# First keys on ScalarE, convolution steps ahead of turns, feed-forward bias two pairs later

## The chip, the core and the metric

The kernel runs on one core of one Trainium2 chip. The metric is the device time of one execution in microseconds (us). Matrix products run on TensorE (PE in the profile, PEld its weight loads), element-wise work on VectorE (DVE), ScalarE (ACT) and GpSimd (POOL); SyncE (SP) issues most of the DMAs. Each engine takes its instructions in the order in which the program was built.

## The reference

The input is x, 2 images of 256 channels on 56 x 56 points, in float32. Two layers act on it:

```python
# layer 0
x = x + conv_attention(group_norm(x))
# layer 1, on tokens of 256 values
t = to_tokens(x)
t = t + attention(layer_norm(t))
t = t + experts(layer_norm(t))
x = from_tokens(t)
```

`conv_attention` makes q, k and v by a 1 x 1 product and a depthwise 3 x 3 convolution, and lets every point attend to a 7 x 7 window (four heads with dilation 1, four with dilation 2), followed by a projection. `attention` is linear attention: with K = elu(k) + 1 and Q = elu(q) + 1 it sums K's products with v over all tokens of an image, and each query reads these sums (the message); a feed-forward net of 512 hidden values with Relu takes token and message. `experts` sends each token to two of eight feed-forward nets with Gelu.

## The kernel before, in words

The first image's convolutions and window attention come first (0 to about 420 us). Then `layer1` runs linear attention in two halves, one for each image; `half == 0` is the first image. Expert work fills gaps from about 795 us on, and is all there is from about 1440 us to the end.

**Keys.** `linear` (L1640) sets up a half. Its tokens are taken in pairs of 128-token tiles (12 pairs and a half tile in each image, `pairs`). `keys` (L266) is a generator with three parts per pair. Part one: statistics of the tile (`stats`, L246; its rstd is a VectorE instruction, L260, and a power on GpSimd, L261), the normalised tile xt (`norm`, L154, on VectorE), its turn by four transposes into pts (L278), copied to xT on ScalarE or VectorE by turns (`evac`, L178). Then up holds the scale and offset with which ScalarE changes t in place (L289); GpSimd adds b2 (L292). Part two: kp from xT and w_k (L297), and ks = elu(kp) + 1 by two ScalarE instructions (L242, L243) and one on VectorE (L244). Part three: kx adds ks times xt into PSUM (L309), and kacc adds ks on GpSimd (L314, L316). rs, up, st and mv come from a pool with three buffers (the pool `sm`), and so do the xt tiles (tag u); a fourth pair reuses the buffers of the first. For the first three pairs (`j < 3`, eager) norm and evac stand with high priority.

`all_keys` (L2105) yields after each part of each pair, in the order part two of a pair, part one of the next, part three of the one before. Behind yield 5 `layer1` calls `ln.feed()`, which is `prepare_feed_forward` (L1781): it centres fw2 (a sum wmean on VectorE, L1733, and a subtraction, L1735), makes the bias hb by 8 products (L1788), copies it (L1792) and scales two quarters of fw1 (L1794).

**Turns.** `steps` (L2144) then advances groups of four tiles through queries (q: pq and, in its second part, pd and qz), message (m: pm, then mts), feed-forward (f: p and py), routing (r) and scatters (P). Each string of `parts` is a turn; each letter takes the next piece of one of these.

**Convolution steps.** The second image's convolutions are left over as a generator, `Convolutions.run` (L496). A step (`fill` in the keys, letter k in `parts`) is two matmuls into py (L521, 448 or 280 columns), and a ScalarE copy into ypad (L527). Four steps fill one of two ypad halves; then 18 strips of 784 values follow, two on ScalarE (L561) and 16 on VectorE (L564, into yc), and one store of yc to DRAM on SP (L579). py has one PSUM bank, ypad two halves, yc two buffers. The strips have a low priority (LATE).

**What sets the order.** The framework orders the instructions of all engines by priority and by its own estimate of times, except TensorE's: under `manual_schedule` they stand as written, and what an engine has in front of it is fixed when the program is built. `tc.issue_after(x)` places instructions behind x. Loads, stores and spills stand on SP in one queue.

Of the kernel before, what the change touches and what calls it, by code (L numbers as in the profile page):

```python
# [13 lines left out]
F32 = mybir.dt.float32  # L14
AF = mybir.ActivationFunctionType
ALU = mybir.AluOpType
# [4 lines left out]
P = 128  # L21
# [40 lines left out]
NFS, NHS = 48, 5  # L62
NFI = 14
LEAD = 22
ENDING = (4, 6, 13, 15, 20)
XW = C + 4

# [58 lines left out]
def hybrid_kernel(ctx: ExitStack, tc: tile.TileContext, a: dict, out: bass.AP):  # L126
    nc = tc.nc
# [138 lines left out]
    def keys(tk, wk, sm, ps, bank, w_k, b2, kx, acc, n0, n, p, first, last, eager):  # L266


        t = tk.at(n0, n)[p]
        rows = p.stop - p.start  # L270
        mv, rs = stats(sm, t, tk.up[p, n0 : n0 + n], p)
        xt = wk.tile([P, 2, C + E], F32, name="xt", tag="u", bufs=3)[p, :, :C]
        pts = ps.tile([P, 2, 2 * P], F32, name="pts", tag="a")
        for k in range(n):
            with tc.high_priority() if eager else nullcontext():
                norm(xt[:, k, :], t[:, k, :], mv, rs, k)
            for ct in range(2):
                nc.tensor.transpose(  # L278
                    pts[:, ct, k * P : k * P + rows], xt[:, k, ct * P : (ct + 1) * P], ident[p, p]
                )  # L280
        xT = tk.turned(n0, n)[:, :, p] if n == 1 else tk.turned(n0, n)
        with tc.high_priority() if eager else nullcontext():
            evac(xT, pts[:, :, : n * rows])

        up = sm.tile([P, 2, 2], F32, name="up")[p]
        nc.vector.tensor_scalar(up[:, 0, :n], rs[:, :n], 1.0, None, ALU.add)
        nc.vector.scalar_tensor_tensor(up[:, 1, :n], mv[:, :n, 0], -1.0, rs[:, :n], ALU.mult, ALU.mult)
        for k in range(n):
            nc.scalar.activation(  # L289
                t[:, k, :], t[:, k, :], AF.Identity, bias=up[:, 1, k : k + 1], scale=up[:, 0, k : k + 1]  # L290
            )
        nc.gpsimd.tensor_tensor(t, t, b2[p].unsqueeze(1).to_broadcast([rows, n, C]), ALU.add)  # L292
        yield
        kps = bank()[p]
        for k in range(n):
            for ct in range(2):
                nc.tensor.matmul(  # L297
                    kps[:, k, :], xT[:, ct, k * rows : (k + 1) * rows], w_k[:, ct, :],
                    start=(ct == 0), stop=(ct == 1),
                )  # L300
        ks = wk.tile([P, 2, C], F32, name="ks", tag="mn")[p]
        elu1(
            wk, ks[:, :n, :].rearrange("p k c -> p (k c)"), kps[:, :n, :].rearrange("p k c -> p (k c)"),
            "k", 4, p,
        )
        yield
        for k in range(n):
            for hg in range(2):
                nc.tensor.matmul(  # L309
                    kx[:, hg, :], ks[:, k, hg * P : (hg + 1) * P], xt[:, k, :],  # L310
                    start=(first and k == 0 and hg == 0), stop=(last and k == n - 1), skip_group_check=True,
                )
        if first:
            nc.gpsimd.tensor_copy(acc, ks)  # L314
        else:
            nc.gpsimd.tensor_tensor(acc[p, :n, :], acc[p, :n, :], ks[:, :n, :], ALU.add)  # L316
        yield
# [20 lines left out]

    fp = [[dram.tile([KC, NH, 21, wide[s]], F32, name=f"fp{s}{k}") for k in range(3)] for s in range(2)]

    def project(dst, x_t, parts, wpr):

        for ct in range(2):
            nc.tensor.matmul(
                dst[:, ct * P : (ct + 1) * P], x_t[:, ct, :], ident,
                start=(ct == 0), stop=False, is_transpose=True, skip_group_check=True,
            )
        for k, (o, s) in enumerate(parts):
            nc.tensor.matmul(  # L349
                dst, o, wpr[:, s, :], start=False, stop=(k == len(parts) - 1), skip_group_check=True  # L350
            )

    anchors = {}

    def bias_tables(sp, ac, pp):

# [1283 lines left out]
    def linear(ph, tk, half, behind=None):  # L1640
# [11 lines left out]
        kp, sm, tp, wqp, wp, wk, lp = (pools[k] for k in "estqwkl")  # L1652
        ps_a, ps_h, ps_q = pool("p3pa", 2, space=PSUM), pool("p3ph", 3, space=PSUM), pool("p3pq", 2, space=PSUM)
# [12 lines left out]
        with tc.issue_after(anchors["final"]) if behind else nullcontext(), tc.high_priority():  # L1666
            w_k = load("w_k", rows("L1_attn_Wk"), [P, 2, C], kp)
            b2 = load("b2", a["L1_attn_b2"].partition_broadcast(P), [P, C], kp)
# [429 lines left out]
        if half == 0:  # L2098
            kx = ps_h.tile([P, 2, C], F32, name="kx", tag="h")
        else:  # L2100
            kx = ps_k.tile([P, 2, C], F32, name="kx", tag="kx")
        acc = wk.tile([P, 2, C], F32, name="kacc", tag="z")
        pairs = [(n0, 2, slice(0, P)) for n0 in range(first, last, 2)] + [(NA - 1, 1, own)]

        def all_keys():  # L2105


            bank = lambda: (ps_h if half else ps_q).tile(
                [P, 2, C], F32, name="kp", tag="h" if half else "q"
            )  # L2110
            live = {}
            for i in range(len(pairs) + 2):
                for k in (1, 0, 2):
                    j = i - k
                    if j == i and j < len(pairs):
                        live[j] = keys(
                            tk, wk, sm, ps_a, bank, w_k, b2, kx, acc, *pairs[j], j == 0, j == len(pairs) - 1, j < 3
                        )
                    if 0 <= j < len(pairs):
                        next(live[j])  # L2120
                        yield
# [8 lines left out]
        def keep():  # L2130
# [8 lines left out]
            wk=wk, ps_h=ps_h, ps_q=ps_q, ps_a=ps_a, ps_k=ps_k, late=late,  # L2139
            bank=lambda: ps_a.tile([P, 512], F32, name="pp", tag="a"),  # L2140
# [23 lines left out]
    def layer1(whole, tk, conv_ctx=None, conv=None, behind=None):  # L2164
# [5 lines left out]
        def fill(n=1):  # L2170
            for _ in range(n):
                next(conv, None)
# [6 lines left out]
        with ExitStack() as ph:  # L2179
            ln = linear(ph, tk, 0, behind)  # L2180
            with tc.manual_schedule(engines={mybir.EngineType.PE}):
                for i, _ in enumerate(ln.keys()):
                    if i == 5:
                        ln.feed()
                    if i < 3 or (i > 8 and i % 6 == 1):
                        fill()
                merging = ln.close()
                prepared = ln.router()
                parts = (
                    "qkwkxkwkxqwkxqq", "mkqkmkqk", "mkqkfmqffkfkff",  # L2190
                    "mqfkfPPPPmkqfkrfrff", "mqfkpPPPPfmqfrfrff", "mqfpPPPPfmqfrfrff",
                    "mfpPPPPfmfrfrff", "fpPPPPffrffrf", "rpPPPPr", "pPPPP",
                )
                todo = steps(ln, order[:early1], parts, {"k": conv, "w": merging, "x": prepared})
                for part in islice(todo, sum(len(t) for t in parts[:7])):
                    pass
                for _ in conv:
                    pass
            ln.keep()
            if conv_ctx:  # L2200
                conv_ctx.close()
            ex = Experts(whole, tk)
            late = ExitStack()
            if run == 0:
                ln.late(late)
            with tc.manual_schedule(engines={mybir.EngineType.PE}):
                for part in islice(todo, len(parts[7]) + 1):
                    pass

            def ending():  # L2210

                next(todo)
                yield
                for part in islice(todo, 4):
                    pass
                next(todo)
                yield
                table = ex.full_tiles(ln.bank()[:, :E], ln.ones)
                next(table)
                next(todo)  # L2220
                yield
                for part in todo:
                    pass
                yield
                for _ in table:
                    pass

            ending = ending()
            if run:
                for _ in ending:  # L2230
                    pass
# [17 lines left out]
        if run == 0:  # L2249
            with ExitStack() as ph:  # L2250
                bank = Banks()
# [7 lines left out]
                with tc.manual_schedule(engines={mybir.EngineType.PE}):  # L2259
                    for i, what in enumerate(att.run()):  # L2260
                        if i in ENDING:
                            next(ending, None)
                        if i == ENDING[-1]:
                            xc = experts()
                        if i >= LEAD and (what == "scores" or what == "values" or what == "end"):
                            with tc.issue_after(anchors["table"]) if first else nullcontext():
# [168 lines left out]
```

## Time and profile before

| | us |
|---|---|
| three runs | 2000.4, 2003.97, 2013.45 |
| median | 2003.97 |
| profiled execution, its own time | 2003.56 |
| its span, first to last instruction | 2001.8 |
| granted TensorE clock, mean | 0.969 |

| stage (us) | PE busy | DVE busy | ACT busy | clock |
|---|---|---|---|---|
| 300 to 400 | 92.57 | 82.98 | 38.62 | 1.00 |
| 400 to 500 | 82.51 | 85.20 | 36.27 | 0.90 |
| 500 to 550 | 44.43 | 44.38 | 20.50 | 0.97 |
| 550 to 600 | 44.91 | 44.83 | 17.12 | 0.93 |
| 600 to 650 | 49.26 | 37.83 | 21.56 | 1.00 |
| 1500 to 1600 | 100.00 | 20.69 | 26.54 | 1.00 |

How to read it: the profile shows one execution. A busy time is the time in which an engine executes; idle time is put down to the instruction that ended the wait. A float32 matmul of the program is two records in the profile. "clock" is the share of full speed that TensorE was granted. In a row of waits the numbers are the total in us, how often, and the longest; in a row of the timeline they are start and length in us, and in brackets the idle time ahead and what ended it. Rows of windows give for each engine busy time and count.

### The profile page before, as it was taken

What the parts mean: (1) busy time and instruction counts of PE and PEld (TensorE: products, weight loads), DVE (VectorE), ACT (ScalarE), POOL (GpSimd) and SP (SyncE); (2) the same over time, 40 slices, a digit from 0 to 9 for tenths busy, and PEclk for the clock granted to TensorE, in tenths of its full rate; (3) what the DMA queues carried; (4) which work ended last, traced back from release to release, by engine and by line L of the source; (5) the groups of instructions that cost most, each with busy time, mean ns of one, the idle gap of its engine ahead of it and who ended that gap; (6) DMA issues with size and microseconds to landing.
All of it is one profiled execution on the core that took longest, in us unless ns stands there. A gap on an engine that the chain in (4) does not pass through costs nothing.

```text
span 2001.8 us, 27731 instructions
## 1 busy us (share of the span) xinstructions
PE 1842.0 (92%) x9996; PEld 1308.3 (65%) x9996; DVE 1094.2 (55%) x2733; ACT 704.5 (35%) x1331; POOL 582.2 (29%) x634
## 2 busy tenths in 40 slices
PE   6999898988889996899989989999899999999996
PEld 3545354556555654566668756567688888888885
DVE  6978988888887746555557434554531212121221
ACT  2333324324434323445536433323322232323332
POOL 4630221025102444111126311445422222222221
PEclk9999999989999996999999999999999999999998
DMA  4753432340001534654474211114577676766995
GB/s 112 160 138 110 133 92 75 111 146 17 25 38 42 157 85 145 193 152 134 129 201 127 56 34 37 48 57 132 156 230 200 188 199 189 198 190 195 299 279 161
DMA packets 200153, 268.85 MB, mean 134 GB/s; under 512 B 30953, under 2 KB 158615, under 8 KB 199761
## 3 DMA queue, kind: packets, MB, share of 16 engines
q1 hardware_dynamic: 167920, 223.95, 37.0%
q0 software_dynamic: 19728, 27.54, 7.5%
q10 hardware_dynamic: 12352, 15.43, 2.2%
q8 instruction: 83, 1.36, 0.3%
q14 instruction: 70, 0.57, 0.1%
HBM read 200.19 MB, written 70.95 MB: 135 GB/s over the span
## 4 chain that ended last, share of the span: by engine, by line
PE 47%; DMA 4%; DVE 4%; ACT 3%; issue 1%; POOL 1%; SPq 0%; ACTq 0%; DVEq 0%; POOLq 0%
PE ph L1600 13%; PE py L1618 13%; PE p L1935 4%; PE x L1618 2%; DMA y<-yt,idi 2%; PE x L1600 2%; PE py L1951 2%; PE po L658 2%; DMA xr<-xs 1%; PE kx L309 1%; PE kp L297 1%; PE x L349 1%; PE pm L1905 1%; PE s_ps L644 1%; PE px L1569 1%
## 5 line engine op out<-in xcount | busy, mean ns | idle before, releaser
L1600 PE MATMUL ph<-xe,w1e 128*128 128x256 f32 (+1 forms) x1448 | 312.1, 371 | 15.3 <-ACT hT L1604 9.4
L1618 PE MATMUL py<-w2e,hT 128*128 128x256 f32 x1392 | 311.5, 379 | 0.0
L1604 ACT ACTIVATE hT<-ph,sv 128x256 f32<-128x256 f32 (+1 forms) x362 | 165.7, 462 | 393.4 <-PE ph L1600 386.1
L1600 PEld LDWEIGHTS ph<-xe,w1e 128*128 128x128 f32 x1448 | 262.6, 191 | 55.0 <-ACT hT L1604 11.2
L1618 PEld LDWEIGHTS py<-w2e,hT 128*128 128x128 f32 x1392 | 260.2, 190 | 33.2 <-issue 0.2
L167 POOL DMA_INDIRECT y<-yt,idi x101 | 160.2, 1587 | 325.4 <-DVE yt L1624 186.9
L571 DVE SCALAR_TENSOR_TENSOR yc<-ypad,w,yc 128x1120 f32<-128x1120 f32 x144 | 202.8, 1412 | 26.4 <-ACT yc L561 18.5
L261 POOL TENSOR_TENSOR rs<-rs,mhalf 128x2 f32<-128x2 f32 (+3 forms) x90 | 72.1, 805 | 323.6 <-DVE rs L260 292.7
L521 PE MATMUL py<-x_sb,wq 128*128 128x448 f32 (+1 forms) x384 | 153.8, 532 | 5.4 <-ACT ypad L527 3.8
L648 ACT ACTIVATE p<-s_ps 112x952 f32<-112x952 f32 (+5 forms) x88 | 102.1, 1160 | 154.6 <-PE s_ps L644 96.0
L1552 DVE CAST idi<-xr 128x2 int32<-128x2 f32 (+1 forms) x53 | 9.8, 184 | 258.6 <-DMA xr<-xs 258.4
L649 DVE TENSOR_TENSOR p<-p,tab 112x952 f32<-112x952 f32 (+5 forms) x88 | 122.0, 1389 | 45.5 <-ACT p L648 39.6
L542 PE MATMUL pc<-ypad,diag 128*128 128x448 f32 x324 | 131.9, 548 | 0.0
L1624 DVE SCALAR_TENSOR_TENSOR yt<-py,eq,yt 128x256 f32<-128x256 f32 x87 | 41.8, 482 | 156.6 <-PE py L1618 156.4
L1582 POOL TENSOR_SCALAR yt<-b2e,eq 128x256 f32<-128x256 f32 x101 | 50.4, 505 | 251.5 <-DMA b2e<-in_L_ffn_b 209.0
L167 POOL DMA_INDIRECT xs<-row,si x98 | 100.5, 1026 | 71.9 <-DVE si L2082 41.9
L521 PEld LDWEIGHTS py<-x_sb,wq 128*128 128x128 f32 x384 | 71.7, 197 | 67.1 <-issue 56.8
L564 DVE SCALAR_TENSOR_TENSOR yc<-ypad,w,yc 128x784 f32<-128x784 f32 x96 | 101.8, 1077 | 4.2 <-ACT yc L561 3.6
L658 PE MATMUL po<-p,v 98*32 98x170 f32 (+5 forms) x960 | 71.2, 379 | 29.1 <-issue 12.6
L542 PEld LDWEIGHTS pc<-ypad,diag 128*128 128x128 f32 x324 | 59.8, 191 | 52.4 <-issue 48.7
L1935 PE MATMUL p<-m2T,fw 128*128 128x512 f32 (+2 forms) x224 | 93.8, 542 | 0.0
L1935 PE MATMUL p<-xT,fw 128*128 128x512 f32 (+1 forms) x208 | 92.7, 568 | 0.0
(391 smaller groups left out, 2891.1 us busy)
## 6 DMA issues: line engine op xcount, KB each, us to landing
w1e<-in_L_ffn_W SPq DMA_DIRECT2D x53, 1024.0 KB
w2e<-in_L_ffn_W SPq DMA_DIRECT2D x53, 1024.0 KB
yd<-yc SPq DMA_DIRECT2D x24, 784.0 KB
ld<-yd SPq DMA_DIRECT2D x28, 448.0 KB
xr<-xs SPq DMA_DIRECT2D x48, 260.0 KB
b2e<-in_L_ffn_b SPq DMA_DIRECT2D x53, 128.0 KB
t<-td SPq DMA_DIRECT2D x12, 512.0 KB
y<-t ACTq DMA_DIRECT2D x24, 256.0 KB
```

The lines of the kernel that those rows point to most:

```text
L167: ins = nc.gpsimd.indirect_dma_start(out=dst[:, :], out_offset=bass.IndirectOffsetOnAxis(ap=index, axis=0), in_=src, in_offset=None, **kw,)
L521: nc.tensor.matmul(py[:, :n, :], self.wq1[:, ct, oc * P : (oc + 1) * P], self.x_sb[:, ct, (q0 + g0) * WW : (q0 + g0 + n) * WW], start=(ct ...
L542: nc.tensor.matmul(pc, diag[:, tap, :], ypad[:, dy : dy + SHARE, dx : dx + WW], start=(tap == 0), stop=(tap == 8),)
L564: nc.vector.scalar_tensor_tensor(yc[:, y0:y1, :], src, w, yc[:, y0:y1, :], ALU.mult, ALU.add)
L571: nc.vector.scalar_tensor_tensor(yc[:, y0:y1, :], src, w, yc[:, y0:y1, :], ALU.mult, ALU.add)
L648: nc.scalar.activation(p[:nk, :, :n], s_ps[:nk, :, :n], AF.Exp)
L649: nc.vector.tensor_tensor(grid(p), grid(p), table[:nk], ALU.mult)
L658: nc.tensor.matmul(dst[hs] if w is None else den[hs], v[:nk, hs] if w is None else w[:nk, :], p[:, h, :, o : o + q.shape[2]], start=first ...
L1600: nc.tensor.matmul(p1, x.w1[:, ct, j * P : (j + 1) * P], x.xe[:, ct, :], start=(ct == 0), stop=(ct == 1),)
L1604: nc.scalar.activation(hT[:, j, :], p1, AF.Gelu, bias=x.sv[:, 4 + j : 5 + j])
L1618: nc.tensor.matmul(py, hT[:, j, h * P : (h + 1) * P], x.w2[:, j, :], start=(j == 0), stop=(j == NJ - 1),)
L1935: nc.tensor.matmul(p1[:, :w], fw1[:, k, oc * P : (oc + 1) * P], rhs, start=(k == 0), stop=(k == 3))
```

## The change

Four things change. The normalised tiles of the first three pairs of the first image are made by ScalarE (Identity with scale rs and offset -mean times rs, which is the second value of up; up's second value is therefore made ahead, in both halves); only these pairs keep the high priority. One convolution step goes ahead of the keys together with the end of the half image in hand, behind the last projection; the others in the keys go in front of the turn of a later pair instead of behind it, and there are nine instead of eight (`FILLS`). In `parts`, the third, fourth and fifth turn lose one step each, and the first and second gain one each, in front of the messages; the ninth step in the keys is the other. `ln.feed()` is called behind yield 11 instead of 5 in the first half.

```diff
--- before.py
+++ after.py
@@ -62,6 +62,7 @@
 NFS, NHS = 48, 5
 NFI = 14
 LEAD = 22
+FILLS = (0, 2, 12, 18, 24, 27, 33)
 ENDING = (4, 6, 13, 15, 20)
 XW = C + 4
 
@@ -271,8 +272,16 @@
         mv, rs = stats(sm, t, tk.up[p, n0 : n0 + n], p)
         xt = wk.tile([P, 2, C + E], F32, name="xt", tag="u", bufs=3)[p, :, :C]
         pts = ps.tile([P, 2, 2 * P], F32, name="pts", tag="a")
+        up = sm.tile([P, 2, 2], F32, name="up")[p]
+        with tc.high_priority() if eager else nullcontext():
+            nc.vector.scalar_tensor_tensor(up[:, 1, :n], mv[:, :n, 0], -1.0, rs[:, :n], ALU.mult, ALU.mult)
         for k in range(n):
-            with tc.high_priority() if eager else nullcontext():
+            if eager:
+                with tc.high_priority():
+                    nc.scalar.activation(
+                        xt[:, k, :], t[:, k, :], AF.Identity, bias=up[:, 1, k : k + 1], scale=rs[:, k : k + 1]
+                    )
+            else:
                 norm(xt[:, k, :], t[:, k, :], mv, rs, k)
             for ct in range(2):
                 nc.tensor.transpose(
@@ -282,9 +291,7 @@
         with tc.high_priority() if eager else nullcontext():
             evac(xT, pts[:, :, : n * rows])
 
-        up = sm.tile([P, 2, 2], F32, name="up")[p]
         nc.vector.tensor_scalar(up[:, 0, :n], rs[:, :n], 1.0, None, ALU.add)
-        nc.vector.scalar_tensor_tensor(up[:, 1, :n], mv[:, :n, 0], -1.0, rs[:, :n], ALU.mult, ALU.mult)
         for k in range(n):
             nc.scalar.activation(
                 t[:, k, :], t[:, k, :], AF.Identity, bias=up[:, 1, k : k + 1], scale=up[:, 0, k : k + 1]
@@ -338,6 +345,8 @@
 
     fp = [[dram.tile([KC, NH, 21, wide[s]], F32, name=f"fp{s}{k}") for k in range(3)] for s in range(2)]
 
+    anchors = {}
+
     def project(dst, x_t, parts, wpr):
 
         for ct in range(2):
@@ -346,11 +355,9 @@
                 start=(ct == 0), stop=False, is_transpose=True, skip_group_check=True,
             )
         for k, (o, s) in enumerate(parts):
-            nc.tensor.matmul(
+            anchors["projected"] = nc.tensor.matmul(
                 dst, o, wpr[:, s, :], start=False, stop=(k == len(parts) - 1), skip_group_check=True
-            )
-
-    anchors = {}
+            ).ins
 
     def bias_tables(sp, ac, pp):
 
@@ -2114,7 +2121,7 @@
                     j = i - k
                     if j == i and j < len(pairs):
                         live[j] = keys(
-                            tk, wk, sm, ps_a, bank, w_k, b2, kx, acc, *pairs[j], j == 0, j == len(pairs) - 1, j < 3
+                            tk, wk, sm, ps_a, bank, w_k, b2, kx, acc, *pairs[j], j == 0, j == len(pairs) - 1, j < 3 and half == 0
                         )
                     if 0 <= j < len(pairs):
                         next(live[j])
@@ -2179,16 +2186,19 @@
         with ExitStack() as ph:
             ln = linear(ph, tk, 0, behind)
             with tc.manual_schedule(engines={mybir.EngineType.PE}):
+                fill()
+                with tc.issue_after(anchors["projected"]) if behind else nullcontext():
+                    fill()
                 for i, _ in enumerate(ln.keys()):
-                    if i == 5:
+                    if i == 11:
                         ln.feed()
-                    if i < 3 or (i > 8 and i % 6 == 1):
+                    if i in FILLS:
                         fill()
                 merging = ln.close()
                 prepared = ln.router()
                 parts = (
-                    "qkwkxkwkxqwkxqq", "mkqkmkqk", "mkqkfmqffkfkff",
-                    "mqfkfPPPPmkqfkrfrff", "mqfkpPPPPfmqfrfrff", "mqfpPPPPfmqfrfrff",
+                    "qkwkxkwkxqwkxqqk", "mkqkmkqkk", "mkqkfmqffkfff",
+                    "mqfkfPPPPmkqfrfrff", "mqfpPPPPfmqfrfrff", "mqfpPPPPfmqfrfrff",
                     "mfpPPPPfmfrfrff", "fpPPPPffrffrf", "rpPPPPr", "pPPPP",
                 )
                 todo = steps(ln, order[:early1], parts, {"k": conv, "w": merging, "x": prepared})
```

## The prediction

> **What bounds the kernel now.** I read the page first: the share of each engine, then the slices.
>
> ```profile
> PE 1842.0 (92%) x9996; PEld 1308.3 (65%) x9996; DVE 1094.2 (55%) x2733; ACT 704.5 (35%) x1331; POOL 582.2 (29%) x634
> ...
> PE   6999898988889996899989989999899999999996
> PEld 3545354556555654566668756567688888888885
> DVE  6978988888887746555557434554531212121221
> ```
>
> TensorE carries the kernel, so a microsecond is gained only where TensorE stands or runs slowly, and only there can the edits act. They touch the keys of the first image, the first turns behind them, and the second image's convolution steps between them: the time from the last projection (419.6) to where TensorE stops waiting (about 580). The ninth to twelfth slice (400 to 600 us) show both engines at 8 tenths. The windows by 10 us:
>
> ```profile
> 420.00:430.00 10.00, 4.61 (x15) 3.38 (x14) 9.45 (x31) 4.23 (x8) 3.92 (x7) 0.76 0.78 238
> 430.00:440.00 10.00, 8.66 (x33) 5.46 (x31) 3.76 (x9) 4.84 (x8) 3.04 (x4) 0.90 0.75 228
> 440.00:450.00 10.00, 8.60 (x34) 7.58 (x35) 9.03 (x14) 2.02 (x4) 2.11 (x1) 0.66 0.31 95
> ...
> 550.00:560.00 10.00, 5.47 (x15) 3.73 (x14) 9.23 (x16) 1.89 (x5) 0.00 (x0) 0.74 0.20 80
> ...
> 590.00:600.00 10.00, 10.00 (x44) 8.13 (x43) 8.96 (x26) 2.85 (x12) 1.58 (x3) 1.00 0.08 26
> ```
>
> The columns are PE, PEld, DVE, ACT, POOL, granted clock, DMA. Where TensorE is short of work VectorE is full, but for 430 to 440, and the clock falls; from 590 TensorE is full. Over 420 to 580 TensorE is busy 133.24 of 160 (26.8 idle), VectorE 137.62 (22.4 idle). The waits of 420 to 580, TensorE first, then VectorE:
>
> ```profile
> PE pts L278 <- DVE xt L154: 12.0, 9, 4.1
> PE pm L1905 <- DVE qz L1879: 4.5, 2, 3.1
> ...
> PE hb L1788 <- DMA g1b<-in_L_attn_b: 2.6, 1, 2.6
> PE pm L1905 <- DVE mw L1735: 2.4, 1, 2.4
> ```
>
> ```profile
> DVE wmean L1733 <- DMA fw<-in_L_attn_W: 6.2, 1, 6.2
> ```
>
> The timeline shows the price of standing:
>
> ```profile
> 424.28 0.67 PE L278 MATMUL pts<-ident,xt 128*128 128x128 f32 x4 [4.06 <-DVE xt L154]
> 426.28 3.78 PE L297 MATMUL kp<-w_k,xT 128*128 128x256 f32 x8 [1.33 <-ACT xT L182]
> ...
> 434.80 1.89 PE L297 MATMUL kp<-w_k,xT 128*128 128x256 f32 x8
> ```
>
> The same eight records take 3.78 after the gap and 1.89 later. Adding all such rows of the stage above their usual length (kp 1.9 and 1.9, py 1.0 and 1.5, hb 1.0 against 1.84 in the second image, pts and kx 1.9 together, pm 1.5 and 3.0) gives 13.7. So the ceiling of the change is 26.8 + 13.7 = 40.5 us, but VectorE has only 22.4 idle, which is the tighter bound.
>
> **What the Trainium skill says.** "TensorE: Matmul & The Clock Gate", Part 1: after an idle window of about 3.4 us the array runs at half clock; the two kp rows agree (3.78 to 1.89). The same page, "Architectural detail": ScalarE and VectorE are strict FIFO; the trace agrees, since in 433.7 to 439.97 VectorE did nothing behind the wmean that waited. "SBUF — State Buffer", "SBUF: two separate sides": VectorE and GpSimd share a port pair, held for a whole instruction; the trace fits, with xt pairs of 0.72 to 2.24 us, and strips (yc L564) of 1.23 on average in the keys against 1.08 from 405 to 660. "ScalarE: Activation LUTs", "Table sets": Identity is in every set, so it needs no load; the trace has Identity (L289) between Relu and Exp in 420 to 460 without one.
>
> **The change, part by part.**
>
> First keys on ScalarE. Six xt leave VectorE: the row at 423.72 gives 3.13 us for six. Six activations come to ScalarE; of the same form and tile, L289's three take 1.58, so 3.2 for six, behind the t_i copy (420.92, 0.58) and the ypad copy that the built order now puts ahead of them. That copy needs the convolution matmul behind the projection (about 420.1 to 421.7), so it ends near 422.4, the first pair is ready near 423.5 and the first turn starts near 423.6 (424.28 before). xT stands behind five activations, at 425.0 to 425.6, and kp starts at 425.7 (426.28). So the move itself gives 0.6 us on TensorE; the rest is the convolution matmul inside the gap (one step 448 wide is 1.5 us) and a clock that need not fall: kp 1.9 shorter. A new wait comes with it: rs and up rotate in threes, and pair 3's to 5's now stand ahead of xT of pair 1 on VectorE, behind ScalarE's t of pairs 0 to 2 (near 429.8 by adding the queue). VectorE arrives near 426.8: about 3.0 idle. Behind it wait xT, hence kp of pair 1 at 430.8 (434.80 before).
>
> The bias. wmean, centring, two scalings and hb (16 records) stand two pairs later; they issue no DMA. The 6.2 of VectorE and 2.6 of TensorE go; by the walk wmean starts near 440.5, just behind fw's landing at 439.97. If that slack of 0.5 is gone, the wait costs what is missing, a microsecond or so. fw1 is needed only in the third turn, 100 us on. The second image keeps its place for the bias; its first keys lose only their priority, and the built order there differs by an exchange of the two up instructions (0.16 each): nothing.
>
> The convolution steps. Each is two matmuls, one ScalarE copy; four of them bring 16 VectorE strips, two ScalarE strips and one store on SP. Nothing is added in number: nine steps instead of eight in the keys, then 6+5+3+2+0 for 5+4+4+3+1. On SP one store now precedes the stash of mw; SP stood 73.9 us on such stores with nothing urgent behind, so it costs nothing; what hides it is that SP's next loads come at 642. The strips do count: in the built order VectorE has 52 strips ahead of the second message's qz instead of 48, at 1.06 each (busy 101.8 over 96 of them).
>
> **The sum**, at the second message (pm, 554.31 before), on VectorE:
> - idle from 420 to there: 134.3 - 110.27 - 4.30 = 19.7. I keep 9.7 of it: the new 3.0, the waits on POOL's pow 2.6, and half of those on ScalarE's results (ks 3.1, qz 3.0, yc 2.3) 4.1. Change: -10.0. Bounds: at least the new 3.0 stays (-16.7); at most it all stays but wmean's, with the 3.0 on top (-3.2).
> - xt: -3.1. Four strips: 4 x 1.06 = +4.2.
> - together -8.9.
>
> From there TensorE sets the pace. Before, six steps of 448 and two of 280 still lay ahead, now three and two: 3 x 1.5 = -4.5. What their absence uncovers: later turns without steps (656 to 700) show only 0.56 before pd, which exists already. The 3.0 of slow pm I leave out, as VectorE is close behind until 590.
>
> Sum -13.4. Behind 660 I see no clock time that the shift could miss: the chain goes on through TensorE to scatters, experts and output, and moves as a whole. Profiled: 2003.56 - 13.4 = 1990.2 (span 2001.8 to 1988.4); the median shown, 2003.97, is 0.4 above it: 1990.6.
>
> **Rivals.**
> A, little gain: VectorE is nearly full, and strips pulled forward plus port clashes take back what the gaps give. For it: the full windows at 480 to 560. Against it: 6.2 + 3.1 go in any case. With only 3.2 less idle: -3.2 - 3.1 + 4.2 - 4.5 = -6.6; with strips at the 1.23 of the keys and clashes on top, nearer 0: 1997 to 2004.
> B, more gain: VectorE always has a strip at hand, so only the new 3.0 stays: -16.7 - 3.1 + 4.2 - 4.5 = -20.1: 1984 (1978 to 1986).
> C, slower: ScalarE's ypad copies block. A copy may overwrite a half image only when VectorE has done its strips of two halves before. In the built order the fifth half's first copy stands at the first message's turn, when VectorE has exactly the 48 strips done that it needs: no slack. Behind it on ScalarE wait m2T, Relu and squares, for which TensorE waits. Each strip late costs 1.06; it decides when the copies stand more than 13.4 us in all, about 13 strips over the last three halves. With two strips late at each of 12 copies (25 us): +12, 2016. Against it: py's waits for ypad are only 0.7 now.
> That the change does not do what it says is excluded by the built orders: xt on ScalarE, hb behind the third kx, nine steps before the last keys.
>
> **How the numbers follow.** Main 0.60 (own range 1986 to 1997, idle kept from 5 to 16), A 0.19, B 0.13, C 0.08. The range 1981 to 2003 leaves out most of C, the edge of A and B's best end. About 1% is what a measurement of this kernel can tell, that is below 1983.9 or above 2024: faster 0.12 (nearly all B), slower 0.05 (C's bad end), same 0.83.
>
> **What would show it.** Right: no PE gap of 4 us near 420 and kp at 1.9; wmean without a DMA wait; pts waits from 12.0 to under 6; pm waits from 6.9 to under 4; VectorE idle 420 to 560 near 10; TensorE's last step near 600 instead of 641; the part behind 660 as long as before. Wrong: ypad copies waiting for VectorE strips, rs or up waiting over 3 us for ScalarE, new waits at qz or u behind strips, or a part behind 660 of another length.

## The result and the profile after

The changed kernel takes 2001.8 us (median) where the kernel before takes 2005.97 in the runs beside it: a ratio of 0.9977, with a 95% interval of 0.9967 to 0.9986. That is 4.6 us less (2.8 to 6.6), not the 13.4 that were forecast; the size is that of rival A, little gain. The profiled execution took 1999.46, with a span of 1997.7.

The part ahead of the change differs between executions by itself: the last projection starts at 419.62 in the trace of before and at 417.90 in that of after, and between 416.1 and 423.1 in all traces of this study. So times in two traces are compared from the start of the last projection (P; "from P" below), and verdicts come from the ratios of many runs.

The page of the kernel after, its shares and slices:

```profile
PE 1838.6 (92%) x9996; PEld 1306.4 (65%) x9996; DVE 1092.6 (55%) x2727; ACT 705.1 (35%) x1337; POOL 581.1 (29%) x634
...
PE   6999898977999987999989989998899999999996
...
DVE  6888988889897555565557434554531212121221
```

VectorE has six instructions less and ScalarE six more, as designed. In the ninth and tenth slice (400 to 500) VectorE went from 8 and 8 to 8 and 9, TensorE from 8 and 8 down to 7 and 7; in the next two (500 to 600) TensorE rose from 8 and 8 to 9 and 9. The first 30 us in windows of 10 us (PE, PEld, DVE, ACT, POOL, clock, DMA):

```profile
420.00:430.00 10.00, 6.54 (x24) 3.67 (x24) 6.11 (x21) 9.68 (x20) 3.15 (x7) 1.00 0.84 253
430.00:440.00 10.00, 6.08 (x19) 5.04 (x20) 7.88 (x13) 1.71 (x3) 4.46 (x4) 0.66 0.70 198
440.00:450.00 10.00, 8.51 (x42) 6.87 (x41) 9.82 (x14) 4.60 (x9) 5.93 (x6) 1.00 0.20 81
```

420 to 430 and 440 to 450 are better off in clock (0.76 and 0.66 before), but a hole has opened at 430 to 440: TensorE 6.08 where it had 8.66, at a clock of 0.66 where it had 0.90. The waits of 420 to 580 name it, TensorE first, then VectorE:

```profile
PE kp L304 <- DVE xT L185: 14.1, 5, 6.2
PE pts L287 <- DVE xt L155: 3.7, 4, 1.8
...
PE pm L1912 <- DVE qz L1886: 1.6, 2, 1.4
```

```profile
DVE ks L245 <- ACT elu_k L244: 3.7, 2, 2.1
DVE up L2053 <- POOL up_t L264: 3.0, 2, 1.9
```

The waits that the forecast named went as it said: pts for xt 12.0 to 3.7, pm 6.9 to 1.6, wmean's 6.2 and hb's 2.6 are gone. But kp now waits 14.1 for xT, so pts and kp together wait longer than before (19.0 for 13.3, ScalarE's xt and xT included). 6.2 of the 14.1 are one gap in the first keys. The other four waits come later, 7.9 in all, and need no keys on ScalarE: the kernel without that part (`no_keys` below) waits 7.5 for xT, in four waits too. VectorE waits 3.0 for up_t (what GpSimd multiplies out behind each power, L264) in an instruction, L2053, that belongs to the router. The timeline of TensorE:

```profile
423.60 1.99 PE L304 MATMUL kp<-w_k,xT 128*128 128x256 f32 x8
425.43 0.60 PE L287 MATMUL pts<-ident,xt 128*128 128x128 f32 x4
425.99 1.77 PE L528 MATMUL py<-x_sb,wq 128*128 128x448 f32 x4
433.92 3.78 PE L304 MATMUL kp<-w_k,xT 128*128 128x256 f32 x8 [6.16 <-DVE xT L185]
```

The first kp is quick now (1.99 against 3.78). The gap of 4.06 at the first turn has moved one pair on and grown to 6.16, and the slow kp with it. On VectorE, in the same microseconds:

```profile
426.03 0.15 DVE L261 TENSOR_SCALAR rs<-mv 128x2 f32<-128x2 f32 x1
427.26 0.17 DVE L2053 TENSOR_SCALAR up<-up_t 128x4 f32<-128x4 f32 x1 [1.08 <-POOL up_t L264]
427.34 0.23 DVE L261 TENSOR_SCALAR rs<-mv 128x2 f32<-128x2 f32 x2
429.49 1.21 DVE L2053 TENSOR_SCALAR up<-up_t 128x4 f32<-128x4 f32 x1 [1.92 <-POOL up_t L264]
430.61 0.15 DVE L277 SCALAR_TENSOR_TENSOR up<-mv,rs 128x2 f32<-128x2 f32 x1
430.68 1.23 DVE L294 TENSOR_SCALAR up<-rs 128x2 f32<-128x2 f32 x1
...
431.90 1.23 DVE L294 TENSOR_SCALAR up<-rs 128x2 f32<-128x2 f32 x1
...
433.19 0.68 DVE L185 COPY xT<-pts 128x512 f32<-128x512 f32 x1
```

and on GpSimd:

```profile
429.41 3.70 POOL L299 TENSOR_TENSOR t<-t,b 128x512 f32<-128x512 f32 x3
```

From the rs of pair 3 to xT of pair 1 VectorE needs 7.2 us for hardly a microsecond of work. 3.0 are two waits of the router's 1 + up_t, which the new order has put here and which needs what GpSimd writes behind its powers. Some 3.2 are three instructions of 1.21 to 1.23 that otherwise take 0.15, all while GpSimd adds b2 to three pairs in a row.

### The profile page after: what moved, and what is told of

It reads as the page before. It is cut to its first block, busy times and chain, and to the rows that moved or that the text cites. A ratio compares the mean times of both kernels' runs of the same rounds, so it can differ in the third digit from the quotient of the medians.

```text
span 1997.7 us, 27721 instructions
## 1 busy us (share of the span) xinstructions
PE 1838.6 (92%) x9996; PEld 1306.4 (65%) x9996; DVE 1092.6 (55%) x2727; ACT 705.1 (35%) x1337; POOL 581.1 (29%) x634
## 4 chain that ended last, share of the span: by engine, by line
PE 68%; DVE 14%; DMA 7%; ACT 4%; issue 3%; POOL 2%; SPq 1%; another core or an unknown queue 0%; ACTq 0%; DVEq 0%; POOLq 0%
PE ph L1607 14%; PE py L1625 13%; PE p L1942 8%; PE po L665 4%; DVE yc L578 4%; PE py L1958 4%; PE py L528 3%; PE x L1625 2%; DMA y<-yt,idi 2%; DVE yc L571 2%; PE x L1607 2%; PE s_ps L651 2%; PE pc L549 2%; PE pm L1912 2%; PE kp L304 1%
## 5 line engine op out<-in xcount | busy, mean ns | idle before, releaser
L665 PE MATMUL po<-p,v 98*32 98x170 f32 (+5 forms) x960 | 69.9, 372 | 29.0 <-issue 12.7
```

The source lines that it names most:

```text
L665: nc.tensor.matmul(dst[hs] if w is None else den[hs], v[:nk, hs] if w is None else w[:nk, :], p[:, h, :, o : o + q.shape[2]], start=first ...
```

## Experiments

Theory 1: this new stall took the gain. Theory 2: VectorE is full, and the strips pulled forward take back what the waits give. All ratios are to the kernel before, in runs of the same hour on the same chip (its medians were 1991 to 2006 in different hours, on different chips); 0.0010 is 2 us. Where two ratios are subtracted, their intervals add to some 4 to 6 us either way.

**Each part alone, and the stall taken away.** `only_keys` is the kernel before with the ScalarE part of the diff; `only_feed` has `i == 11` for `i == 5`; `only_steps` has FILLS, the two fills ahead and the new `parts`.

> The kernel before with the first three pairs of the first image normalised on ScalarE, and nothing else of the change. Theory 1 (a new stall of VectorE in the first keys, where two of the router's small instructions wait for GpSimd and three more run into GpSimd's adds of b2, took the gain): the turn of pair 0 starts earlier, but xT of pair 1 comes no earlier than before, so the time is within 1.5 us of before. Theory 2 (VectorE is full with work, and what counts is the number of strips it has ahead): six xt less are worth their 3.1 us, so 3 to 5 us less than before.

> The kernel before with the bias of the feed-forward at step 11 of the keys in place of step 5, and nothing else. Theory 1: the 6.2 us that VectorE waited for the DMA of fw stood on the path and nothing takes their place here, so 4 to 6 us less than before. Theory 2: VectorE is full, later strips and waits on ScalarE take up what the DMA wait leaves, 0 to 3 us less.

> The kernel before with the convolution steps placed as in the change (two ahead of the first turn, nine in the keys, fewer in the third group), and nothing else. Theory 1: four more strips ahead of the second message cost 4.2 us there, three steps less behind it give 4.5, and the gap at the first turn is filled with one step: 0 to 3 us less than before. Theory 2: the strips stand ahead of the keys' turns on VectorE and cost more than the 1.08 us of one each, so 1 to 4 us more than before.

`both_behind` is the changed kernel with two edits (`added` is GpSimd's add of the keys, kacc):

```diff
-            nc.vector.tensor_scalar(up, tk.up[:, n0 : n0 + n], 1.0, None, ALU.add)
...
             with tc.issue_after(last.ins):
                 nc.vector.tensor_copy(row[:, :n, C], dest[:, n0 : n0 + n])
+                nc.vector.tensor_scalar(up, tk.up[:, n0 : n0 + n], 1.0, None, ALU.add)
...
-        nc.gpsimd.tensor_tensor(t, t, b2[p].unsqueeze(1).to_broadcast([rows, n, C]), ALU.add)
+        if not eager:
+            nc.gpsimd.tensor_tensor(t, t, b2[p].unsqueeze(1).to_broadcast([rows, n, C]), ALU.add)
...
+        if eager:
+            with tc.issue_after(added.ins):
+                nc.gpsimd.tensor_tensor(t, t, b2[p].unsqueeze(1).to_broadcast([rows, n, C]), ALU.add)
```

> The changed kernel with two sources of the new stall taken away: the router's 1 + up_t (line 2053) stands behind the copies of its rows, which come a hundred microseconds later, and GpSimd adds b2 to the first three pairs only behind its add of the keys of the same pair. Theory 1: VectorE no longer waits 3.0 us for up_t and its three small instructions take 0.15 to 0.2 us each instead of 1.2, so xT of pair 1 comes about 5 us earlier and 3 to 5 us of it reach the end: 7 to 10 us less than before, 3 to 5 less than the changed kernel. Theory 2: the waits are filled from strips that have to be done in any case, so the kernel is within 1.5 us of the changed one (3 to 6 us less than before).

Measured: `only_keys` 1.0009 (0.9997 to 1.0021), `only_feed` 0.9977 (0.9966 to 0.9988), `only_steps` 0.9993 (0.9979 to 1.0006), `both_behind` 0.9939 (0.9922 to 0.9955). `only_feed` and `only_steps` lie where theory 1 put them, `only_keys` just outside (+1.8 for at most 1.5), and `both_behind` gives more than it asked for: 12 us less than before. Theory 2 is contradicted in `only_keys`, hardly fits `only_steps`, and fails in `both_behind`, which keeps the strips where the change put them. So it is not the strips that took the gain. `only_keys` by itself doesn't speak for theory 1, though: there wmean waits for the DMA of fw (the feed-forward's weights) as before, and that alone can take up what the keys give, as `keys_up1` below shows. The three parts add up (+1.8 - 4.6 - 1.4 = -4.2) to what the whole change measured, within their intervals.

**The two sources apart.** `up1_behind` has the first edit of `both_behind` alone, `b2_behind` the second alone, `after_again` is the changed kernel, `no_keys` the changed kernel without its ScalarE part.

> The changed kernel once more, so that the next three stand beside it in runs of the same hour. Both theories: 0.9977 of before again, 3 to 6 us less than before; its chain in the first keys as before, with xT of pair 1 some 7 us behind the rs of pair 3 on VectorE.

> The changed kernel with only the router's 1 + up_t (line 2053) moved behind the copies of its rows; GpSimd's adds of b2 stay where they are. Theory 1a (the waits of VectorE for up_t are the larger part of the new stall): the 3.0 us go, but the three small instructions still wait for GpSimd's pow, 2 us, so xT of pair 1 comes 1 to 3 us earlier; 2 to 4 us less than the changed kernel. Theory 1b (the collisions with the adds of b2 are the larger part): within 1.5 us of the changed kernel.

> The changed kernel with only GpSimd's adds of b2 of the first three pairs moved behind the adds of their keys; the router's 1 + up_t stays ahead of xT on VectorE. Theory 1a: VectorE still waits 3.0 us for up_t, three small instructions fall from 1.2 to 0.15 us each, so xT of pair 1 comes 3 us earlier; 1 to 3 us less than the changed kernel. Theory 1b: 4 to 7 us less than the changed kernel, about what both moves gave together (0.9939 of before).

> The changed kernel without its first part: the first three pairs are normalised on VectorE as before; bias and steps stay moved. Theory 1: the part on ScalarE is worth nothing as it stands (alone it measured 1.0009 of before), so this one is at 0.9977 - 0.0009 or lower: 5 to 7 us less than before, 0 to 3 less than the changed kernel. Theory 2 (with the steps ahead of the turns ScalarE's part does save the 3.1 us of six xt on VectorE): 2 to 4 us more than the changed kernel.

Measured: `after_again` 0.9971 (0.9958 to 0.9983), `up1_behind` 0.9932 (0.9908 to 0.9956), `b2_behind` 0.9953 (0.9940 to 0.9966), `no_keys` 0.9979 (0.9966 to 0.9991). So moving the router's instruction alone is worth about 8 us, moving the adds about 4, hardly clear of the noise, and both together (0.9939, in the hour before) no more than the first. The two edits overlap: with the first the adds begin so late that they miss VectorE's small instructions, so it takes the collisions away too. Both are worth more than theory 1a said; its order isn't shown, as the difference (0.0021) is within the noise. In the traces kp of pair 1 starts 16.0 and 15.7 from P in the changed kernel, 12.7 in `b2_behind`, 12.1 in `both_behind`, 11.6 in `up1_behind`. `no_keys` cannot be told from the changed kernel; it has no wait for up_t either, and is 9 us slower than `up1_behind`, so the keys on ScalarE do pay once the stall is gone and the other parts are there. In the timeline of VectorE of `up1_behind`, the stretch above reads:

```profile
429.56 0.30 DVE L261 TENSOR_SCALAR rs<-mv 128x2 f32<-128x2 f32 x3
430.52 0.16 DVE L277 SCALAR_TENSOR_TENSOR up<-mv,rs 128x2 f32<-128x2 f32 x1 [0.67 <-POOL rs L262]
430.60 0.19 DVE L294 TENSOR_SCALAR up<-rs 128x2 f32<-128x2 f32 x1
...
432.36 0.16 DVE L277 SCALAR_TENSOR_TENSOR up<-mv,rs 128x2 f32<-128x2 f32 x1 [0.65 <-POOL rs L262]
...
432.53 0.68 DVE L185 COPY xT<-pts 128x512 f32<-128x512 f32 x1
```

3.0 us from rs to xT in place of 7.2: three waits of 0.65 to 0.67 for GpSimd's powers, and quick instructions, since GpSimd's adds now begin at 432.55, behind them. TensorE's second kp follows after a gap of 0.67, and takes 1.99 instead of 3.78. In `b2_behind` the waits for up_t are still there (1.08 and 1.93), but not the collisions; its VectorE, behind the second wait:

```profile
434.55 0.15 DVE L277 SCALAR_TENSOR_TENSOR up<-mv,rs 128x2 f32<-128x2 f32 x1
434.62 0.17 DVE L294 TENSOR_SCALAR up<-rs 128x2 f32<-128x2 f32 x1
...
434.97 0.69 DVE L185 COPY xT<-pts 128x512 f32<-128x512 f32 x1
```

**A control, and each part taken back out.** `before_up1` is the kernel before with the first edit. The other three are `up1_behind` with the bias at yield 5, with the old fills and `parts`, and with one step of the keys moved to the third group:

```diff
-FILLS = (0, 2, 12, 18, 24, 27, 33)
+FILLS = (0, 2, 12, 18, 27, 33)
...
-                    "qkwkxkwkxqwkxqqk", "mkqkmkqkk", "mkqkfmqffkfff",
+                    "qkwkxkwkxqwkxqqk", "mkqkmkqkk", "mkqkfmqffkfkff",
```

> Control: the kernel before with the router's 1 + up_t moved behind the copies of its rows, nothing else. Theory 1 (these instructions cost only because the change put them ahead of xT on VectorE while GpSimd had not written up_t; before they stood at 431.7 without a wait): within 1.5 us of before. Rival (moving them frees VectorE by itself and has nothing to do with the change): 4 to 8 us less than before.

> The changed kernel with the router's 1 + up_t moved (0.9932 of before), and the bias of the feed-forward back at step 5 of the keys. Theory 1 with the prediction's sum: wmean then stands on VectorE before fw has landed and waits at least the 6.2 us that it waited before, so 4 to 8 us more than with the bias at step 11. Rival (strips and keys are short enough elsewhere that the wait is made up): within 2 us of it.

> The changed kernel with the router's 1 + up_t moved, and the convolution steps placed as before (eight in the keys, none ahead of the first turn). The prediction's sum: four strips less ahead of the second message give 4.2 back there, three steps more behind it cost 4.5, so within 2 us of the kernel with the steps moved. Rival (steps fill TensorE's gaps in the keys and cost nothing on VectorE): 3 to 6 us more than with the steps moved. Theory 2 (strips pulled forward are what costs): 3 to 6 us less.

> The changed kernel with the router's 1 + up_t moved and one step of the nine in the keys moved to the third group of the messages: in the built order 47 strips stand ahead of the second message's qz instead of 52. The prediction's sum: five strips less are 5.3 us there, one step of 448 more behind it costs 1.5, so 3 to 4 us less than with nine steps. Rival (VectorE is not the bound there, TensorE waits for other things): 0 to 2 us more.

Measured: `before_up1` 0.9994 (0.9977 to 1.0011), so moving the router's instruction is worth nothing by itself; the change made it costly. `up1_old_bias` 0.9990 (0.9973 to 1.0006), `up1_old_steps` 0.9977 (0.9965 to 0.9990), `up1_8steps` 0.9980 (0.9965 to 0.9994). In `up1_old_bias` wmean waits 5.0 for fw again and hb 4.0 for g1b. Against `up1_behind` of the hour before, each takes back 9 to 12 us, where I expected 4 to 8 for the bias, about none for the steps, and even a gain for eight steps. Here my sum failed a second time.

**Whether that lies in the hours.** Two of these again, beside `up1_again` (the same as `up1_behind`), and `keys_up1`, which is `only_keys` with the first edit:

> The changed kernel with the router's 1 + up_t moved, once more, beside the three that follow. If the steps carry the gain: 0.993 of before again, 11 to 16 us less. If the earlier ratio came from too few runs: 0.996 to 0.998.

> Eight steps in the keys and one more in the third group, once more. In the traces so far it was 1.7 us later than the kernel with nine at the second message and 6.6 later at the last routed group. If that is what the step does: 4 to 8 us more than the kernel with nine. If the hours differed: within 3 us of it.

> Keys and bias as changed, 1 + up_t moved, steps as before, once more. If strips fill VectorE's waits in the keys: 6 to 10 us more than with the steps moved (0.9977 of before again). By the prediction's sum: within 2 us of it.

> The kernel before with the keys on ScalarE and the router's 1 + up_t moved, bias and steps as before. If the keys pay by themselves once the stall is gone: 3 to 6 us less than before. If the landing of fw sets the time (wmean, on VectorE, waits for it at step 5 whatever stands ahead): within 2 us of before.

Measured: `up1_again` 0.9928 (0.9906 to 0.9949), `up1_8steps_again` 0.9950 (0.9939 to 0.9961), `up1_old_steps_again` 0.9968 (0.9958 to 0.9979), `keys_up1` 1.0003 (0.9990 to 1.0015). The best kernel stands: 14 us less than before, about 9 less than the change. The steps carry 8 of the 14. The ninth step is worth about 4 here, which is no more than the noise, and 10 by the earlier ratios across two hours; how much exactly stays open. `keys_up1` gains nothing, as expected if the landing of fw sets the time; its VectorE waits:

```profile
DVE wmean L1739 <- DMA fw<-in_L_attn_W: 5.3, 1, 5.3
```

The sums of VectorE from P to the second message (the start of its last fourteen records, 556.45 before; the prediction's 554.31 is its first two; the rows of windows cut at these two times; idle is length less busy) show what the parts do to each other:

| kernel | length | DVE busy | DVE idle |
|---|---|---|---|
| before | 136.83 | 117.10 | 19.7 |
| before_up1 | 133.91 | 113.42 | 20.5 |
| after | 135.51 | 120.61 | 14.9 |
| after_again | 134.12 | 120.52 | 13.6 |
| up1_behind | 128.61 | 118.26 | 10.3 |
| up1_again | 130.46 | 118.59 | 11.9 |
| up1_8steps | 130.30 | 113.39 | 16.9 |
| up1_8steps_again | 126.50 | 112.57 | 13.9 |
| up1_old_steps | 132.42 | 112.46 | 20.0 |
| up1_old_steps_again | 132.36 | 111.07 | 21.3 |
| up1_old_bias | 141.68 | 118.00 | 23.7 |

With the old steps VectorE has 6 to 7.5 us less to do and waits 8 to 11 longer, mostly for ScalarE. Its longest such waits from 418 to 560, first in `up1_old_steps`, then in `up1_behind`:

```profile
DVE yc L571 <- ACT yc L568: 4.2, 3, 1.9
DVE rs L261 <- ACT sq L1806: 3.5, 3, 1.5
DVE ks L245 <- ACT elu_k L244: 3.4, 3, 1.8
DVE qz L245 <- ACT elu_q L244: 3.3, 3, 1.5
```

```profile
DVE rs L261 <- ACT sq L1806: 2.2, 3, 1.4
DVE ks L245 <- ACT elu_k L244: 1.6, 1, 1.6
...
DVE yc L571 <- ACT yc L568: 1.3, 3, 0.5
DVE qz L245 <- ACT elu_q L244: 0.7, 2, 0.5
```

Strips pulled forward fill such waits. The waits for GpSimd's powers hardly change (2.6 and 2.5).

With eight steps VectorE has 5 to 6 us less to do and waits 2 to 7 longer, and the second message comes, on the whole, no later than with nine (130.30 and 126.50 against 128.61 and 130.46). What the eighth loses stands behind it: 191.4 and 191.3 us from there to the last routed group, against 186.5 and 184.9. The expectation had only 1.5 there. In `up1_8steps` TensorE waits for m2T at the third message's turn, where VectorE has five strips to do first. In `up1_again` there are two, and the gap is 0.85.

```profile
607.28 1.72 PE L1881 MATMUL pd<-qz,ksm 128*128 128x512 f32 x2 [4.07 <-DVE m2T L185]
```

```profile
601.31 5.31 DVE L571 SCALAR_TENSOR_TENSOR yc<-ypad,w,yc 128x784 f32<-128x784 f32 x5
606.54 0.68 DVE L185 COPY m2T<-mts 128x512 f32<-128x512 f32 x1
```

## Why the prediction was wrong

**The step that failed** is the new wait in "First keys on ScalarE": "rs and up rotate in threes, and pair 3's to 5's now stand ahead of xT of pair 1 on VectorE, behind ScalarE's t of pairs 0 to 2 (near 429.8 by adding the queue). VectorE arrives near 426.8: about 3.0 idle." This counted rs and up alone, and put at nothing what else stands ahead of that xT: the router's two 1 + up_t, and GpSimd's adds of b2, which VectorE meets there. I had read the built order for rs and up and passed over the other two.

The wait for t is real and was placed well. In `up1_behind`, where nothing else stands there, ScalarE's t of pair 2 ends at 432.26, 10.6 from P (10.2 forecast), and VectorE's last up starts at 432.36, behind GpSimd's power, which ends only 0.07 later than t:

```profile
430.67 1.59 ACT L296 ACTIVATE t<-t,up 128x256 f32<-128x256 f32 x3
```

```profile
431.63 0.69 POOL L262 TENSOR_TENSOR rs<-rs,mhalf 128x2 f32<-128x2 f32 x1
```

In the kernel before, the two 1 + up_t stood behind all of these, without a wait:

```profile
431.73 0.80 DVE L2046 TENSOR_SCALAR up<-up_t 128x4 f32<-128x4 f32 x2
```

In the changed kernel they wait 3.0 (that this is the length forecast for another wait is chance), and hold VectorE until GpSimd's adds have begun, which cost another 3.2. So the stretch took 7.2, and kp of pair 1 starts 16.0 from P (433.92 less 417.90), later than before (15.2); the forecast was 11.2 (430.8 less 419.6), and `up1_behind` has 11.6. What was forecast ahead of it came: the first turn starts 3.3 from P (4.0 forecast), the first kp 5.7 (6.1), and it is 1.8 shorter (1.9).

**The sum at the second message**, forecast -8.9 from before's 136.8. After: idle -4.8 for -10.0, busy +3.5 for +1.1, together -1.3 (-2.7 in `after_again`). `up1_behind`: idle -9.4, busy +1.2, together -8.2 (-6.4 in `up1_again`). Without the stall the forecast of the idle time kept came true: 9.7 forecast, 10.3 measured; with it, 14.9. One caution: `before_up1`, whose time is that of before, has 133.91 in place of 136.83, so a single execution is good to some 3 us here, and it is the ratios that decide. That busy agrees in `up1_behind` is luck: the strips cost 9.3 more there (63.5 for 54.2), 5 more than was booked, and small savings that nobody booked make it up (the instructions that write up alone take 9.0 before and 6.8 there).

**The strips.** The count was right (53 records of 784 for 49), the price not: 62.4 for 54.2 us in the changed kernel, 8.2 in place of 4.2. The mean of all rose from 1.125 to 1.188. The traces show where: a strip with no GpSimd work beside it takes 1.02 to 1.04, and each of the strips that take 1.25 to 2.01 (8 before, 11 after) does so while GpSimd adds or copies. Four more strips are 4.1; the three more of the long strips, and their greater length, are the other 4. The prediction had 1.23 for the strips in the keys and booked 1.06 all the same. But to book them as a cost beside an idle time that shrinks was wrong as well: the idle time shrinks in part because of them. Without the moved steps it stays at 20.0 and 21.3.

**Steps behind the second message**, forecast -4.5 for three steps: from there to the last routed group 191.1 before, 186.4 after, 186.5 in `up1_behind`. The size came, but not from the steps alone: the fourteen records of pm at its start take 5.84 before and 3.29 after, a term that the sum left out, so the steps' own part is less. The last step starts at 605.75 (forecast near 600).

**The bias.** wmean at 448.09 with no DMA wait, hb 1.84 long without one: right. Alone it is worth 4.6 us, and in `keys_up1`, without it, the keys give nothing even with the stall gone.

**Behind 660.** From the last routed group to the end the trace of before has 1254.3, that of after 1257.8; over all traces it is 1244 to 1261, and it differs by 8 between two executions of one kernel in different hours (1253.7 in `up1_behind`, 1245.5 in `up1_again`). It neither confirms nor excludes a loss of some microseconds there; this stays open. That the traces of after and `after_again` have the longest ends of their hours may be more than chance, but `only_keys`, which has the stall too, has the shortest of its hour.

**Rivals.** A came true in size, and in its port clashes: 3.2 in the stall and about 4 in the strips. That the strips as such take the gain back did not come: with the same strips `up1_behind` gains 14. B did not come: it asked for 16.7 less idle time, and the most that any kernel shows is 9.4. C did not come: TensorE's wait for ypad was 1.9 in all.

## What to carry to other kernels

Where an edit changes what a scheduler sees as free time, read the whole built order ahead of the instruction that the next engine waits for, not only the instructions that the edit is about: here two unrelated ones of 0.15 us that needed a late result cost about 8 us. Work that is pulled forward into an engine's waits isn't a cost to be added to the idle time that it fills; and parts of such a change (here the keys and the steps) can be worth nothing alone and 8 to 9 us in company.

## What the runs showed of the hardware

The Trainium skill ("SBUF — State Buffer", "SBUF: two separate sides") says that a VectorE instruction in a two-port mode, or with two SBUF inputs beside a GpSimd instruction that reads SBUF, and that GpSimd instruction take turns at a shared port pair, each for its whole length. The traces agree in the waiting; in which mode an instruction ran they don't show. Unexpected was the size for a small one: a VectorE instruction on 128 x 2 values took 1.23 us in place of 0.15 while GpSimd ran adds of 128 x 512 (1.25 to 1.26 each), so it waited for about a whole add, and three of them in a row met three adds. The three end at 430.70, 431.92 and 433.13, each 0.02 to 0.03 behind the end of an add. With the adds moved away (`b2_behind`) the same ones took 0.17. It goes both ways: the same three adds took 3.70 us in the changed kernel and 5.19 in `up1_behind`, where they fell beside strips, and two strips beside them took 3.40, where one strip alone takes 1.02 to 1.04:

```profile
432.55 5.19 POOL L299 TENSOR_TENSOR t<-t,b 128x512 f32<-128x512 f32 x3
```

```profile
435.18 3.40 DVE L571 SCALAR_TENSOR_TENSOR yc<-ypad,w,yc 128x784 f32<-128x784 f32 x2
```

The clock also fell behind a gap shorter than the 3.4 us that the prediction cites (2.30), and did not behind a longer one (3.08). The eight records of kp in `only_steps`, then in the changed kernel:

```profile
472.34 3.58 PE L298 MATMUL kp<-w_k,xT 128*128 128x256 f32 x8 [2.30 <-DVE xT L185]
```

```profile
484.66 2.00 PE L304 MATMUL kp<-w_k,xT 128*128 128x256 f32 x8 [3.08 <-DVE xT L185]
```

So the length of the gap just ahead doesn't tell by itself, and what else decides isn't shown.
